# Sums of 32-row strips through DRAM, in place of one-hot matmuls, in a graph layer

## The chip, the cores and the metric

One core of a Trainium2 chip runs the kernel. The metric is the device time of one execution in microseconds (us).

## The reference

A graph layer over 6250 nodes and 206,250 edges (33 per node), D = 256, all in float32. The edges come sorted by their target node `dst`.

```python
h = relu(layernorm(x))                                   # [6250, 256]
e = relu(edge_attr[:, 1:] @ W_e1.T + b_e1) @ W_e2.T + b_e2
edge_emb = (e * (clip(edge_attr[:, 0:1], 0, 1) + 0.01)) @ W_le.T + b_le
msg = relu(h[src] + edge_emb)                            # per edge
aggr = segment_sum(msg, dst, 6250)                       # per node
y = (h + aggr) @ W_g1.T + b_g1
out = x + relu(layernorm(y) * ln_g + ln_b) @ W_g2.T + b_g2
```

## The kernel before

**Edges.** A tile is 128 edges. A block is S = 4 tiles, a half-block (the loop's unit `u`) two of them, a pair `q` two blocks. A group is L = 6 blocks, 3072 edges; its edges are laid out so that tile j of each of its blocks belongs to strip j, a run of 768 consecutive edges. The targets of such a run lie within W = 32 consecutive nodes. There are 67 full groups and at the end an odd one of one block (403 blocks, 806 half-blocks).

**Per half-block** the steps are these. `first_layer` (line 250) multiplies the edge features by `W_e1`, per pair; `edge_part` (L274) multiplies the result by the product of `W_e2` and `W_le`, and DVE copies it out as `msg` (L279). GpSimd (POOL) gathers the rows of `hb` = h + b_le by `src`, 128 rows in one indirect DMA (L566), two gathers per half-block, 1604 in the main part. `whole` multiplies `msg` by the polarity and adds the gathered rows (L615, DVE), then takes the relu (L620, ACT). `add_up` multiplies by 0/1 matrices `sel` (L632): strip j of the group is summed in partitions 32j to 32j+31 of an accumulator `pd`.

**Per group**, `keep` copies the accumulator to `ms` (L644, 128 rows x 256): 4 strips of 32 rows, each row the sum of one node over this group's edges.

**Per window** of 128 nodes (49 of them), `node_work` puts the groups' sums in their places and ends the layer. A window takes sums from two or three groups; there are 140 pairs of window and group. Its steps:

- `spread` loads x, x transposed (`hT`) and the rows' statistics (`stb`), and builds a one-hot matrix per group (L698); small steps on DVE turn `hT` into h (L707) and prepare `xt` (L211).
- `rows_of` (L732) multiplies each group's `ms` by its one-hot matrix, which gives the sums already transposed, and DVE adds h (L734).
- `one` is the product with `W_g1` (L170) and the normalisation, `two` the transposes (L186) and the relu (L189), `three` the product with `W_g2` (L196), the sum with x (L198) and the store (L201).

**Order.** The schedule is written by hand; each engine runs its instructions in the order in which the program emits them. The main loop counts half-blocks `u` from LEAD = 22 (22 are calculated before the first gather can run). `edge_part(u)` comes first; at each turn (every eight half-blocks) come `add_pairs` (all sums that are possible) and two `first_layer` calls and the raw loads of the pairs for the turn after (SP). `whole` follows `edge_part` at a distance `lag`, which starts at 18 half-blocks and gets shorter by one every 44. Node steps stand in `todo` with a due half-block, and `due` runs at most one per half-block.

**The gathers' account.** `in_step` books a fixed time for each step of PE and emits gathers as long as their number fits; the first of them waits for that step's last matmul (`behind`). What is still missing when `whole` needs it is emitted there, without such a wait.

```python
EDGE, LAYER, SUMS, NODES = 1.754, 0.9, 0.46, 0.65
STEP = 1.288
AFLOAT = 6.0
    spent += us
    while (got - 2 * RAW) * STEP < spent + AFLOAT and got < 2 * min(NU, 4 * summed + HG):
        gather(behind)
        behind = None
```

`EDGE` is booked per half-block, `LAYER` twice per `first_layer`, `SUMS` per block in `add_up`, `NODES` per step that `due` runs. `gathers(made + 1)` is the untied way.

**A fallback.** `verdict` and the steps around it test whether the targets lie as the layout assumes; if not, `any_order` computes everything again in a general way.

Of the kernel before, what the change touches and what calls it, by code (L numbers as in the profile page):

```python
# [17 lines left out]
P = 128  # L18
N = 6250
# [14 lines left out]
NB = NF * L + 1  # L34
NT = NB * S
NG = NF + 1
NP = -(-NB // 2)
MARGIN = 768
DEG = E // N
# [12 lines left out]
AHEAD = 10  # L52
assert DEG * N == E and NF * GE + S * P >= E


def group_of(b):
    return b // L


def blocks_of(g):  # L60
    return range(g * L, min((g + 1) * L, NB))


def windows_of(g):

    lo = (GE * g - MARGIN) // DEG
    hi = (GE * (g + 1) + MARGIN) // DEG
    return [w for w in range(NW) if w * P <= hi and (w + 1) * P > lo]
# [29 lines left out]
def gnn_kernel(ctx: ExitStack, tc: tile.TileContext, x, src_c, dst_c, dst_r, pol_c, raw_t, w_e1t, w_e2,  # L98
# [6 lines left out]
    st_d = dram.tile([NW, 2, P], F32, name="st_d")  # L105

# [42 lines left out]
    def finish_nodes(nd, ps, w, n):  # L149
# [3 lines left out]
        def turn(a):  # L153
# [3 lines left out]
            aT = nd.tile([P, 2, P], F32, name="aT")  # L157
# [7 lines left out]
        def first(aT, bias_by_pe=False):  # L165
            ph = ps()
            if bias_by_pe:
                nc.tensor.matmul(ph[:n, 0, :], ones[0:1, :n], bg1_b[0:1], start=True, stop=False)
            for c in range(2):
                nc.tensor.matmul(ph[:n, 0, :], aT[:, c, :n], wg1_s[:, c, :], start=c == 0 and not bias_by_pe, stop=c == 1)  # L170
            hs = nd.tile([P, D], F32, name="hs")
            if bias_by_pe:
# [7 lines left out]
            nc.vector.tensor_scalar(hs[:n], hb[:n], mv[:n, 0, 0:1], rs[:n], op0=ALU.subtract, op1=ALU.mult)  # L180
# [32 lines left out]
        return turn, first, second, third, load_x, offset  # L213
# [4 lines left out]
    with fast:  # L218
# [20 lines left out]
        def first_layer(q):  # L239

            bs = [b for b in (2 * q, 2 * q + 1) if b < NB]
# [97 lines left out]
        nc.gpsimd.iota(mid, pattern=[[GE, NG]], base=GE // 2, channel_multiplier=0, allow_small_or_imprecise_dtypes=True)  # L339
        p32 = const.tile([P, 1], F32, name="p32")  # L340
# [9 lines left out]
        full = NF * L * S  # L350
# [134 lines left out]
        def first_rows():  # L485

            pb = ps().rearrange("p a b -> p (a b)")[:, :NG * S].rearrange("p (g j) -> p g j", j=S)
            nc.tensor.matmul(pb[:, :NF, :], ones[0:1, :],
                             dst_f[0:1, :full].rearrange("o (g r) -> o g r", r=L * S)[:, :, :S], start=True, stop=True)
            nc.tensor.matmul(pb[:, NF, :], ones[0:1, :], dst_f[0:1, full:], start=True, stop=True)  # L490
            nc.scalar.activation(base_b, pb, AF.Copy)

        def rows_of_edges():
# [3 lines left out]
                base_b[:, :NF, :].rearrange("p g (o j) -> p g o j", o=1).to_broadcast([P, NF, L, S]), ALU.subtract)  # L497
            nc.vector.tensor_tensor(rel[:, full:], dst_f[:, full:], base_b[:, NF, :], ALU.subtract)
# [10 lines left out]
        def row_numbers():  # L509
            for j in range(S):  # L510
                q = slice(j * W, (j + 1) * W)
                nc.vector.tensor_scalar(rowid[q], base_b[q, :, j], p32[q], None, op0=ALU.add)


        far = w0.tile([P, 2, NG], F32, name="far")
        ends = w0.tile([P, 3], F32, name="ends")
        bad = w0.tile([P, 3], F32, name="bad")
        bad3 = w0.tile([3, 1], F32, name="bad3")

        def by_group(i, op):  # L520
            def step():
                nc.vector.tensor_reduce(far[:, i, :NF], dst_f[:, :full].rearrange("p (g r) -> p g r", r=L * S),
                                        axis=AX.X, op=op)
                nc.vector.tensor_reduce(far[:, i, NF:], dst_f[:, full:], axis=AX.X, op=op)
# [6 lines left out]

        def verdict():
            nc.vector.scalar_tensor_tensor(far[:, 0, :], far[:, 0, :], float(DEG), mid, op0=ALU.mult, op1=ALU.subtract)
            nc.vector.scalar_tensor_tensor(far[:, 1, :], far[:, 1, :], -float(DEG), mid, op0=ALU.mult, op1=ALU.add)
            nc.vector.tensor_reduce(ends[:, 2:3], far.rearrange("p a b -> p (a b)"), axis=AX.X, op=ALU.max)
            nc.vector.tensor_scalar(bad[:, 0:1], ends[:, 0:1], float(W - 1), None, op0=ALU.is_gt)
            nc.vector.tensor_scalar(bad[:, 1:2], ends[:, 1:2], 0.0, None, op0=ALU.is_lt)
            nc.vector.tensor_scalar(bad[:, 2:3], ends[:, 2:3], float(GE // 2 + MARGIN), None, op0=ALU.is_gt)

        def count():  # L540
            pq = ps()
            nc.tensor.matmul(pq[:3, 0, 0:1], bad, ones[:, 0:1], start=True, stop=True)
            nc.vector.tensor_copy(bad3, pq[:3, 0, 0:1])

        def total():
            pq = ps()
            nc.tensor.matmul(pq[:1, 0, 0:1], bad3, ones[0:3, 0:1], start=True, stop=True)
# [3 lines left out]
        with tc.tile_pool(name="hg", bufs=HG - RAW) as hg_p, tc.tile_pool(name="ms", bufs=5) as ms_p, \  # L551
                tc.tile_pool(name="sel2", bufs=9) as sel2_p, tc.tile_pool(name="nd", bufs=3) as nd:
# [6 lines left out]
            def gather(behind=None):  # L559

                nonlocal got
                u, i = divmod(got, 2)
                got += 1
                if i == 0:
                    hg[u] = (hx_p if u % HG < RAW else hg_p).tile([P, 2, D], F32, name="hg")
# [12 lines left out]
            def in_step(us, behind):  # L578
# [3 lines left out]
                while (got - 2 * RAW) * STEP < spent + AFLOAT and got < 2 * min(NU, 4 * summed + HG):  # L582
# [7 lines left out]
            def rows_of_block(g, k):  # L590

                t = (g * L + k) * S
# [7 lines left out]
            def piece():  # L600

                if steps and steps[0][0] <= now:
                    steps.popleft()[1]()
# [18 lines left out]
            def add_up(b):  # L622

                g = group_of(b)
                k = b - g * L
                if k == 0:
                    acc[g] = pd[:, g % 2, :] if g < NG - 1 else ps()[:, 0, :]
# [11 lines left out]
            def keep(g):  # L639

                if g is not None:
                    ms[g] = ms_p.tile([P, D], F32, name="ms")
                    if g != NG - 2:
                        nc.scalar.activation(ms[g], acc.pop(g), AF.Copy)  # L644
                    else:
                        nc.vector.tensor_copy(ms[g], acc.pop(g))
                    sel.pop(g)
                    for w in range(NW):
                        if groups_of(w)[-1] == g:
                            late.pop(w)()  # L650
                        elif groups_of(w)[-1] == g + 1 < NG - 1:
                            late[w] = node_work(w)

            def add_pairs(last=False):
# [3 lines left out]
                while summed < NP and min(4 * summed + 4, NU) < made + last:  # L658
                    for b in (2 * summed, 2 * summed + 1):
                        if b < NB:  # L660
                            whole_groups.append(add_up(b))
                            if b % L == 0 and group_of(b) + 2 < NG:
# [12 lines left out]
            ending = {-2: [], -1: []}  # L675
# [4 lines left out]
            def node_work(w, spread_now=False):  # L680
# [4 lines left out]
                far_apart = (3, 5, 4) if gs[-1] < NG - 3 else (2, 3, 2)  # L685
                turn, first, second, third, load_x, offset = finish_nodes(nd, ps, w, n)

                def spread():
                    box["xt"] = load_x()
                    box["hT"] = nd.tile([P, 2, P], F32, name="hT")  # L690
                    nc.sync.dma_start(out=box["hT"][:, :, :n], in_=x_t[:, :, w * P:w * P + n])
                    st = nd.tile([P, 2, P], F32, name="stb")
# [25 lines left out]

                def halves_out():
# [6 lines left out]
                def rows_of():  # L726
# [9 lines left out]
                    if gs[-1] < NG - 2:  # L736
                        at(now + far_apart[0], one)

                def one():
                    box["hs"] = first(box["hT"], gs[-1] >= NG - 2)  # L740
                    if gs[-1] < NG - 2:
                        at(now + far_apart[1], two)

                def two():
                    box["nT"] = second(box["hs"])
                    if gs[-1] < NG - 2:
# [9 lines left out]
                if gs[-1] < NG - 2:  # L756
                    return lambda: at(now + 2, rows_of)
                ending[gs[-1] - NG].append((sums_of, halves_out, rows_of, one, two, three, gs))
# [19 lines left out]
            for i, fn in ((0, first_rows), (1, strips), (5, row_numbers), (6, stats_out),  # L778
                          (8, node_weights)):
                at(LEAD + i, fn)  # L780
            for i, fn in enumerate((by_group(0, ALU.max), by_group(1, ALU.min), by_row(0, ALU.max), by_row(1, ALU.min),
                                    verdict, count, total)):
                at(LEAD + 22 + 5 * i, fn)
            flag = None
            for u in range(LEAD, NU):
                now = u
                forward(u)
# [7 lines left out]
                while made < ready_for:  # L795
                    gathers(made + 1)
                    whole(made)
                    made += 1
                due()
                if len(rest) > 6:  # L800
# [5 lines left out]
                if u == LEAD + 60:  # L806
                    flag = nc.values_load(bad_i[0:1, 0:1], min_val=0, max_val=3 * P)
# [4 lines left out]
            while steps:  # L812
                steps.popleft()[1]()
            before, last = ending[-2], ending[-1]
            for sums_of, halves_out, rows_of, one, two, three, gs in before:
                rows_of()
            for sums_of, halves_out, rows_of, one, two, three, gs in last:
                sums_of(gs[:-1])
            while made < NU:
                whole(made)  # L820
                made += 1
            for sums_of, halves_out, rows_of, one, two, three, gs in before:
                one()
            add_pairs(last=True)
            for sums_of, halves_out, rows_of, one, two, three, gs in last:
                sums_of(gs[-1:])
                halves_out()
            for sums_of, halves_out, rows_of, one, two, three, gs in before:
                two()
            for sums_of, halves_out, rows_of, one, two, three, gs in last:  # L830
                one()
            for sums_of, halves_out, rows_of, one, two, three, gs in before:
                three()
            for sums_of, halves_out, rows_of, one, two, three, gs in last:
# [10 lines left out]
def any_order(tc, dram, v):  # L845
# [7 lines left out]
    with tc.tile_pool(name="sc", bufs=1) as sc, tc.tile_pool(name="sk", bufs=2) as sk, \  # L853
# [78 lines left out]
        def nodes(w, n):  # L932
            ac = sk.tile([P, D], F32, name="ac_a")
            nc.sync.dma_start(out=ac[:n], in_=acc_d[bass.ds(w * P, n), :])
            turn, one, two, three, load_x, offset = v["finish_nodes"](sk, lambda: sp1.tile([P, 1, D], F32, name="ps_a"), w, n)
# [71 lines left out]
```

## Time and profile before

| | |
|---|---|
| median of 3 runs | 2162.19 us (2161.35 to 2164.05) |
| the profiled execution: its own time | 2161.02 us |
| its span, first to last instruction | 2159.3 us |
| granted TensorE clock, mean | 0.998 |
| PE (TensorE) busy | 2144.8 us |
| DVE (VectorE) busy | 1665.9 us |
| ACT (ScalarE) busy | 980.5 us |
| POOL (GpSimd) busy | 1621.5 us |
| DMA, mean rate | 143 GB/s |

A row of the profile gives line, engine, operation, out<-in by the program's names, the number of instructions, then busy time and the mean of one in ns, then the engine's idle time ahead of them and what ended it. PEld is the weight load. Names with a q (SPq, POOLq) are queues: instructions that issue DMAs or wait. In a row of a line with times by stretch, the columns are the stretch, its length, the busy time with the number of instructions, the granted clock, the DMA engines' share and GB/s. A float32 matmul stands as two instructions, a transpose as one.

### The profile page before, as it was taken

The numbers are of one execution on the slowest core, as the hardware profiler recorded it, in microseconds if no ns is written. First come the engines' busy times: TensorE is split into PE (matmuls) and PEld (weight loads), VectorE is DVE, ScalarE is ACT, GpSimd is POOL, SyncE is SP. The second block draws the span as 40 slices with busy tenths as digits, with TensorE's granted clock in tenths as the row PEclk, the third lists the DMA queues.
The fourth block names the chain that finished last, engine by engine and source line by source line (L and its number), as shares of the span: only waits on it lengthen the run. The fifth ranks groups of instructions, "written<-read, shape, count | busy, mean of one in ns | idle before, by whom it ended". The sixth has DMA issues, their size and how long they took to land.

```text
span 2159.3 us, 35666 instructions
## 1 busy us (share of the span) xinstructions
PE 2144.8 (99%) x12382; PEld 1613.3 (75%) x12382; DVE 1665.9 (77%) x3975; ACT 980.5 (45%) x1710; POOL 1621.5 (75%) x1675
## 2 busy tenths in 40 slices
PE   9999999999999999999999999999999999999998
PEld 6677777777777777777777777777777777777776
DVE  7898777877777777777777777778777778777786
ACT  7544444444444444444444444444444444444443
POOL 6777777777777777777777777777777777777773
PEclk9999999999999999999999999999999999999999
DMA  9544454544445454545454445444544554454442
GB/s 312 175 134 127 141 157 135 150 137 131 140 131 148 144 149 125 152 131 149 124 151 142 133 130 153 143 133 141 147 138 125 150 151 140 128 152 131 140 138 73
DMA packets 156227, 309.23 MB, mean 143 GB/s; under 512 B 33328, under 2 KB 78089, under 8 KB 156041
## 3 DMA queue, kind: packets, MB, share of 16 engines
q0 software_dynamic: 77376, 211.39, 34.6%
q1 hardware_dynamic: 77364, 92.23, 13.6%
q10 hardware_dynamic: 1300, 3.28, 0.5%
q8 instruction: 98, 1.61, 0.3%
q14 instruction: 89, 0.72, 0.1%
HBM read 293.92 MB, written 12.85 MB: 142 GB/s over the span
## 4 chain that ended last, share of the span: by engine, by line
PE 96%; DVE 2%; DMA 1%; ACT 0%; issue 0%; SPq 0%; DVEq 0%; ACTq 0%
PE pz L274 64%; PE pz L250 17%; PE pd L632 9%; PE pz L732 3%; PE pz L170 2%; PE pz L196 2%; DMA raw<-in_raw_t_dram 1%; PE pz L186 1%; DVE hg L615 0%; DVE msg L279 0%; DVE st L141 0%; DMA xt<-in_x_dram 0%; DVE sel L595 0%; DVE mvx L142 0%; DVE msg L613 0%
## 5 line engine op out<-in xcount | busy, mean ns | idle before, releaser
L566 POOL DMA_INDIRECT hg<-hb_d,src_s x1604 | 1576.6, 983 | 493.9 <-issue 319.8
L274 PE MATMUL pz<-wc_s,e 128*128 128x256 f32 x6448 | 1452.6, 381 | 0.0
L274 PEld LDWEIGHTS pz<-wc_s,e 128*128 128x128 f32 x6448 | 1209.5, 190 | 235.2 <-ACT e L259 71.3
L620 ACT ACTIVATE hg<-hg 128x512 f32<-128x512 f32 x805 | 507.6, 631 | 862.7 <-DVE hg L615 860.9
L615 DVE SCALAR_TENSOR_TENSOR hg<-msg,pol_s,hg 128x256 f32<-128x256 f32 x1612 | 696.8, 477 | 15.6 <-DMA hg<-hb_d,src_s 14.9
L279 DVE TENSOR_TENSOR msg<-pz,bc_s 128x512 f32<-128x512 f32 x799 | 545.5, 683 | 74.0 <-PE pz L274 73.7
L256 DVE TENSOR_SCALAR e<-pz,vecs 128x512 f32<-128x512 f32 x201 | 150.8, 750 | 361.1 <-PE pz L250 361.0
L259 ACT ACTIVATE e<-pz,vecs 128x512 f32<-128x512 f32 x605 | 361.1, 691 | 148.4 <-PE pz L250 148.3
L250 PE MATMUL pz<-raw,we_s 64*128 64x512 f32 x1612 | 379.3, 604 | 3.7 <-DVE msg L279 2.0
L250 PEld LDWEIGHTS pz<-raw,we_s 64*128 64x128 f32 x1612 | 148.5, 187 | 188.2 <-issue 155.4
L632 PE MATMUL pd<-hg,sel 128*32 128x256 f32 x3216 | 194.9, 382 | 0.6 <-ACT hg L620 0.6
L632 PEld LDWEIGHTS pd<-hg,sel 128*32 128x32 f32 x3216 | 94.4, 109 | 87.8 <-issue 34.9
L595 DVE SCALAR_TENSOR_TENSOR sel<-iota_w,zero_c,rel 128x128 f32<-128x128 f32 x403 | 137.3, 341 | 0.0
L644 ACT ACTIVATE ms<-pd 128x256 f32<-128x256 f32 x66 | 25.2, 382 | 127.2 <-PE pd L632 127.1
L732 PEld LDWEIGHTS pz<-s,ms 128*128 128x128 f32 x548 | 68.7, 192 | 3.1 <-PE pd L632 0.4
L732 PE MATMUL pz<-s,ms 128*128 128x128 f32 x548 | 69.3, 275 | 0.1
L707 DVE SCALAR_TENSOR_TENSOR hT<-hT,zero_c,stb 128x128 f32<-128x128 f32 (+1 forms) x196 | 66.7, 341 | 3.0 <-DMA stb<-st_d 3.0
L196 PE MATMUL pz<-wg_s,nT 128*128 128x256 f32 (+1 forms) x196 | 50.6, 380 | 0.6 <-ACT nT L189 0.6
L170 PE MATMUL pz<-wg_s,hT 128*128 128x256 f32 (+1 forms) x196 | 50.5, 380 | 0.0
L392 POOL TENSOR_TENSOR hb<-xt,rows_b 128x256 f32<-128x256 f32 (+1 forms) x49 | 34.1, 728 | 10.5 <-ACT xt L388 3.0
L196 PEld LDWEIGHTS pz<-wg_s,nT 128*128 128x128 f32 (+1 forms) x196 | 37.0, 190 | 6.2 <-ACT nT L189 0.8
L170 PEld LDWEIGHTS pz<-wg_s,hT 128*128 128x128 f32 (+1 forms) x196 | 37.0, 190 | 5.7 <-issue 0.3
(98 smaller groups left out, 412.8 us busy)
## 6 DMA issues: line engine op xcount, KB each, us to landing
raw<-in_raw_t_dram SPq DMA_DIRECT2D x202, 256.0 KB
hg<-hb_d,src_s POOLq DMA_INDIRECT x1604
stb<-st_d SPq DMA_DIRECT2D x49, 128.0 KB
hb_d<-hb SPq DMA_DIRECT2D x12, 512.0 KB
xt<-in_x_dram SPq DMA_DIRECT2D x48, 128.0 KB
hT<-in_x_t_dram SPq DMA_DIRECT2D x48, 128.0 KB
out_dram<-ot SPq DMA_DIRECT2D x48, 128.0 KB
xt<-in_x_dram SPq DMA_DIRECT2D x11, 512.0 KB
```

Source lines behind the costliest of these rows:

```text
L196: nc.tensor.matmul(po[:n, 0, :], nT[:, c, :n], wg2_s[:, c, :], start=c == 0, stop=c == 1)
L250: z = nc.tensor.matmul(pe[s, c], we1_s[s * F:(s + 1) * F, c * P:(c + 1) * P], raw[q][s * F:(s + 1) * F, :], start=True, stop=True)
L256: nc.vector.tensor_scalar(e1[b][:, c, :], pe[s, c], be1_s[:, c:c + 1], 0.0, op0=ALU.add, op1=ALU.max)
L259: nc.scalar.activation(e1[b][:, c, :], pe[s, c], AF.Relu, bias=be1_s[:, c:c + 1])
L274: last_z = nc.tensor.matmul(pz[:, i, :], e1[b][:, c, k:k + P], wc_s[:, c, :], start=c == 0, stop=c == 1)
L279: nc.vector.tensor_add(msg[u], pz, bc_s)
L566: g = nc.gpsimd.indirect_dma_start(out=hg[u][:, i, :], out_offset=None, in_=hb_d, in_offset=bass.IndirectOffsetOnAxis(ap=src_s[:, 2 * u + ...
L595: nc.vector.scalar_tensor_tensor(sel[g][:, k * S:(k + 1) * S, :], iota_w.rearrange("p (o w) -> p o w", o=1).to_broadcast([P, S, W]), zero_ ...
L615: nc.vector.scalar_tensor_tensor(hg[u][:, i, :], m[:, i, :], pol_s[:, 2 * u + i:2 * u + i + 1], hg[u][:, i, :], op0=ALU.mult, op1=ALU.add)
L620: nc.scalar.activation(hg[u], hg[u], AF.Relu)
L632: z = nc.tensor.matmul(acc[g][j * W:(j + 1) * W, :], sel[g][:, k * S + j, :], m[:, j % 2, :], start=k == 0, stop=b == blocks_of(g)[-1])
L732: nc.tensor.matmul(pa[:, c, :n], ms[g][:, c * P:(c + 1) * P], box["sel2"][i][:, :n], start=i == 0, stop=i == len(gs) - 1)
```

## The change

Two things change.

**Sums through DRAM.** For the windows whose last group is before the odd one (47 of 49), `rows_of` and its one-hot matrices go. Two DRAM tables `sum_d[0]`, `sum_d[1]` of N + 32 rows are cleared window by window (`clear`). After a group's copy, `rows_out` loads the first node numbers of its four strips into SP's registers and stores the strips to these rows, even strips in one table and odd ones in the other. `far_work` takes the place of `node_work`: x is loaded, ACT computes h (`load`), SP loads 128 rows of both tables, DVE adds them (`add`, twice), `turned` transposes on PE and copies out on ACT; `one`, `two` and `third` follow as before. `turned`, `one`, `two` and `third` are run by `due`; the rest isn't: SP's part is started by `moves` at fixed distances of 1 to 8 half-blocks.

**The odd group.** The block of the odd group moves ahead of the last full group, next to a void block (VOID) that is skipped everywhere; 404 blocks, 808 half-blocks in number, 806 of them computed. At the end only the last window is left; its first groups' sums and its bias are begun ahead of the last blocks.

The test gets one more condition (strips two apart don't overlap). EDGE, LAYER, SUMS, NODES, STEP, AFLOAT, `lag` and `due` stay as they are. The core of the diff:

```diff
+CLEAR = 4
 def group_of(b):
-    return b // L
+    return b // L if b < VOID else NG - 1
...
+    sum_d = [dram.tile([N + W, D], F32, name=f"sum_d{i}") for i in range(2)]
...
+            nc.vector.tensor_copy(base_i, base_b[0:1].rearrange("p g j -> p (g j)"))
...
             def gather(behind=None):
                 nonlocal got
+                if got == 4 * VOID:
+                    got += 4
...
-                while (got - 2 * RAW) * STEP < spent + AFLOAT and got < 2 * min(NU, 4 * summed + HG):
+                while (got - 4 * (got > 4 * VOID) - 2 * RAW) * STEP < spent + AFLOAT and got < 2 * min(NU, 4 * summed + HG):
...
             def keep(g):
...
                     sel.pop(g)
+                    if g < FAR:
+                        soon(1, lambda: rows_out(g, 0))
+                        soon(2, lambda: rows_out(g, 1))
                     for w in range(NW):
-                        if groups_of(w)[-1] == g:
+                        if groups_of(w)[0] == g + CLEAR:
+                            soon(6, lambda w=w: clear(w))
+                        if groups_of(w)[-1] == g < FAR:
+                            far_work(w)
+                        elif groups_of(w)[-1] == g:
                             late.pop(w)()
...
+            def soon(n, fn):
+                moves.setdefault(now + n, []).append(fn)
+
+            def clear(w):
+                if groups_of(w)[-1] < FAR:
+                    for i in range(2):
+                        nc.sync.dma_start(out=sum_d[i][w * P:(w + 1) * P, :], in_=zrow)
+
+            def rows_out(g, k):
+                if k == 0:
+                    _, firsts[g] = nc.values_load_multi_w_load_instructions(
+                        base_i[0:1, g * S:(g + 1) * S], engines=[mybir.EngineType.SP], min_val=0, max_val=N)
+                for i in range(2):
+                    j = 2 * k + i
+                    nc.sync.dma_start(out=sum_d[i][bass.ds(firsts[g][j], W), :], in_=ms[g][j * W:(j + 1) * W, :])
+
+            def far_work(w):
+                box = {}
+                turn, bias, first, second, third, load_x, offset = finish_nodes(nd, ps, w, P)
+                def h_of_x():
+                    box["xt"] = load_x()
+                    box["h"] = nh.tile([P, 2, P], F32, name="stb").rearrange("p a b -> p (a b)")
+                def load():
+                    nc.scalar.activation(box["h"], box["xt"], AF.Relu, bias=nm_s[:, w:w + 1], scale=rs_s[:, w:w + 1])
+                    box["ab"] = ab_p.tile([P, 2, D], F32, name="ab")
+                    for i in range(2):
+                        nc.sync.dma_start(out=box["ab"][:, i, :], in_=sum_d[i][w * P:(w + 1) * P, :])
+                def add(i):
+                    nc.vector.tensor_add(box["h"], box["h"], box["ab"][:, i, :])
+                def turned():
+                    box["hT"] = turn(box["h"], nh, "hT")
+                    at(now + 2, one)
+                def one():
+                    box["hs"] = first(box["hT"])
+                    at(now + 5, two)
+                def two():
+                    box["nT"] = second(box["hs"])
+                    at(now + 4, lambda: third(box["nT"], box["xt"]))
+                soon(1, h_of_x)
+                soon(4, load)
+                steps.extend((now + 6, lambda i=i: add(i)) for i in range(2))
+                steps.extend((now + 7, lambda c=c: offset(box["xt"], c)) for c in range(2))
+                at(now + 9, turned)
...
             for u in range(LEAD, NU):
                 now = u
-                forward(u)
+                if u == NU - 1:
+                    whole(made)
+                    made += 1
+                if u // 2 != VOID:
+                    forward(u)
...
                 due()
+                for fn in moves.pop(now, []):
+                    fn()
...
+            for begin, sums_of, halves_out, one, two, three, gs in ending:
+                begin()
+            while made < NU:
+                whole(made)
+                made += 1
...
+            add_pairs(last=True)
+            for begin, sums_of, halves_out, one, two, three, gs in ending:
+                sums_of(gs[-1:])
+                halves_out()
+                one()
```

More of the change, by code (lines that the diff above doesn't have):

```diff
@@ L37 @@
 NP = -(-NB // 2)
+FAR = NG - 2
 MARGIN = 768
+SP = S * P
+LAST = 512
+VOID = (NF - 1) * L + 1
 DEG = E // N
@@ L211, in offset @@
             nc.vector.scalar_tensor_tensor(xt[:n, h], xt[:n, h], zero_c[:n], bg2_b[:n, h], op0=ALU.add, op1=ALU.add)
-        return turn, first, second, third, load_x, offset
+        return turn, bias, first, second, third, load_x, offset
     NU = 2 * NB
@@ L600, in piece @@
             def piece():
-                if steps and steps[0][0] <= now:
-                    steps.popleft()[1]()
+                due_now = [s for s in steps if s[0] <= now][:1]
+                if due_now:
+                    steps.remove(due_now[0])
+                    due_now[0][1]()
                 elif rest:
@@ L806, in gnn_kernel @@
                 if u == LEAD + 60:
-                    flag = nc.values_load(bad_i[0:1, 0:1], min_val=0, max_val=3 * P)
+                    flag = nc.values_load(bad_i[0:1, 0:1], min_val=0, max_val=4 * P)
+            assert not moves
+            while steps:
+                steps.popleft()[1]()
+            for begin, sums_of, halves_out, one, two, three, gs in ending:
+                begin()
+            while made < NU:
+                whole(made)
+                made += 1
+            for now in sorted(todo):
+                for fn in todo.pop(now):
+                    fn()
+            add_pairs(last=True)
[3 more added lines that the diff above has]
+                one()
             while todo:
@@ L811, in gnn_kernel @@
                     fn()
[L812 to L834, printed above, removed]
+            for begin, sums_of, halves_out, one, two, three, gs in ending:
                 two()
```

167 lines of the change are left out of this document (107 added, 60 removed).

## The prediction

> **What bounds the kernel now.** I read the page first (the shares of the engines, the chain that ended last), then the groups of instructions by line, then one line alone (the gathers) with its table by stretches, then the timeline at the places that carry a price.
>
> ```profile
> span 2159.3 us, 35666 instructions
> PE 2144.8 (99%) x12382; PEld 1613.3 (75%) x12382; DVE 1665.9 (77%) x3975; ACT 980.5 (45%) x1710; POOL 1621.5 (75%) x1675
> PE 96%; DVE 2%; DMA 1%; ACT 0%; issue 0%; SPq 0%; DVEq 0%; ACTq 0%
> PE pz L274 64%; PE pz L250 17%; PE pd L632 9%; PE pz L732 3%; PE pz L170 2%; PE pz L196 2%; DMA raw<-in_raw_t_dram 1%; PE pz L186 1%; DVE hg L615 0%; DVE msg L279 0%; DVE st L141 0%; DMA xt<-in_x_dram 0%; DVE sel L595 0%; DVE mvx L142 0%; DVE msg L613 0%
> ```
>
> By the page TensorE (PE) is the bound: busy for 99% of the span and 96% of the chain. GpSimd (POOL) seems to have a quarter to spare. Its one large line says otherwise:
>
> ```profile
> L566 POOL DMA_INDIRECT hg<-hb_d,src_s x1604 | 1576.6, 983 | 493.9 <-issue 319.8 <-PE pz L274 41.2 <-ACT hg L620 32.9
> L566 POOL DMA_INDIRECT hg<-hb_d,src_s x1604: 942/946/1963, 65.3 to 2131.8; - x179
> 100.00:200.00 100.00, 76.55 (x78) 1.00 0.49 142
> 1200.00:1300.00 100.00, 76.23 (x79) 1.00 0.46 133
> 2000.00:2100.00 100.00, 75.91 (x78) 1.00 0.48 141
> 263.08 0.94 POOL L566 DMA_INDIRECT hg<-hb_d,src_s  x1 [0.30 <-PE pz L196]
> 265.86 0.48 DVE L615 SCALAR_TENSOR_TENSOR hg<-msg,pol_s,hg 128x256 f32<-128x256 f32 x1 [0.77 <-DMA hg<-hb_d,src_s]
> 2131.85 0.95 POOL L566 DMA_INDIRECT hg<-hb_d,src_s  x1 [0.30 <-issue]
> ```
>
> The first gather starts at 65.3 us, the last ends at 2131.85 + 0.95 = 2132.8. That is 2067.5 us for 1604 gathers, 1.289 us each, and 78 or 79 of them in every 100 us, early and late. The idle time of 493.9 us is 0.308 us a gather, and 0.30 stands ahead of a gather even where nothing held it (the last row); only some 10 us of it can be waiting. So POOL is full as well, from 65.3 to 2132.8. The kernel has two full engines, and the page's share hides the second because the gap of 0.30 isn't counted as busy. A faster PE alone can't move the end of the gathers.
>
> The Trainium skill, "Trainium Kernel Development and Optimization" (Performance Expectations), says that matmul busy time tells badly how near a kernel is to its limit and that LDWEIGHTS busy is the better measure. Here that is 75% beside 99%, so by that rule a cut on PE is worth less than its own length; by PE's 99% it is worth all of it (the third rival). The gathers' rows agree with the rule.
>
> **PE: what goes and what comes.** A window of 128 nodes now costs a one-hot matmul per group that reaches into it. In the code there are 140 such pairs; 47 windows with 134 of the pairs take the new path, and the last two windows keep the old one.
>
> ```profile
> L732 PE MATMUL pz<-s,ms 128*128 128x128 f32 x548 | 69.3, 275 | 0.1
> 1005.94 1.93 PE L632 MATMUL pd<-hg,sel 128*32 128x256 f32 x32
> 1007.80 3.70 PE L250 MATMUL pz<-raw,we_s 64*128 64x512 f32 x16
> 1011.44 3.72 PE L274 MATMUL pz<-wc_s,e 128*128 128x256 f32 x16
> 1015.00 1.50 PE L732 MATMUL pz<-s,ms 128*128 128x128 f32 x12
> 1016.33 5.35 PE L274 MATMUL pz<-wc_s,e 128*128 128x256 f32 x24
> 1036.71 0.38 PE L186 MATMUL pz<-ident,hs 128*128 128x128 f32 x2
> 1036.93 1.89 PE L274 MATMUL pz<-wc_s,e 128*128 128x256 f32 x8
> ```
>
> Twelve instructions (three groups) take the stream from 1015.00 to 1016.33: 0.111 us each. 134 pairs are 536 instructions: 59.4 us go. Two transposes a window come; two of them take from 1036.71 to 1036.93, 0.22 us: 47 x 0.22 = 10.3 us. PE gets 49 us shorter. The edge matmuls, the first layer and the strips' sums are the same in number (the void block is skipped), and so are the 1604 gathers.
>
> **DVE, ACT and SP.**
>
> ```profile
> L615 DVE SCALAR_TENSOR_TENSOR hg<-msg,pol_s,hg 128x256 f32<-128x256 f32 x1612 | 696.8, 477 | 15.6 <-DMA hg<-hb_d,src_s 14.9
> L707 DVE SCALAR_TENSOR_TENSOR hT<-hT,zero_c,stb 128x128 f32<-128x128 f32 (+1 forms) x196 | 66.7, 341 | 3.0 <-DMA stb<-st_d 3.0
> L698 DVE TENSOR_SCALAR s<-iota_p,rowid 128x128 f32<-128x128 f32 x140 | 31.6, 289 | 0.0
> L734 DVE SCALAR_TENSOR_TENSOR hT<-hT,pz 128x256 f32<-128x256 f32 x48 | 19.6, 409 | 0.0
> L388 ACT ACTIVATE xt<-xt,nm_s,rs_s 128x256 f32<-128x256 f32 (+1 forms) x49 | 25.4, 590 | 7.1 <-DVE nm_s L385 6.9
> L644 ACT ACTIVATE ms<-pd 128x256 f32<-128x256 f32 x66 | 25.2, 382 | 127.2 <-PE pd L632 127.1
> L620 ACT ACTIVATE hg<-hg 128x512 f32<-128x512 f32 x805 | 507.6, 631 | 862.7 <-DVE hg L615 860.9 <-DVE ot L198 1.5 <-DVE bad L543 0.3
> SPq L201 <- DVE ot L198: 1383.9, 48, 36.6
> L807 SPq TENSOR_LOAD <-bad_i x1: 485/485/485, 216.8 to 216.8; - x1
> L807 SPq FUSED_REGOPS  x1: 181/181/181, 217.3 to 217.3; - x1
> L201 SPq DMA_DIRECT2D out_dram<-ot x49: 333/344/344, 195.3 to 2154.0; - x49
> ```
>
> DVE loses 188 x 0.34 (L707) + 134 x 0.23 (L698) + 47 x 0.41 (L734) = 114 us and gains 94 additions of 128x256; the nearest row is L615, 696.8/1612 = 0.43 us, so 41 us: 73 us less on an engine that isn't the bound. ACT gains 47 x (0.59 + 0.38) = 46 us (a relu like L388, a copy out of PSUM like L644) and had 45%. Both cost nothing while PE and POOL are full.
>
> SP gets, for each of 66 groups, four register loads (0.49 + 0.18 us each, row L807) and four stores (0.34 each), and per window two clears and two loads of sums in place of two other loads. On SP's queue a store now waits for the group's sums, and loads of sums wait for stores. Queued behind it stand the raw loads, whose users come eight half-blocks later (a half-block is 256 edges, two gathers, 2.6 us; so 21 us); SP already sits in such waits for 1383.9 us. The chain from a group's copy to the loaded sums, with the landing time below for each transfer that waits for another: 0.4 + 2.7 + 0.7 + 1.8 + 0.7 + 1.8 + 0.9 + 1.8 = 10.8 us; DVE adds six half-blocks, 15.6 us, after it. Cover of 5 us: I take no cost. Without it DVE stalls, and that is a rival.
>
> **The step that decides: what paces the gathers.** A gather is put into POOL's program by an account: each PE step books a fixed time (1.754 per half-block, 0.9 twice per pair, 0.46 per block, 0.65 per node step), and gathers are emitted, tied to that PE step, as long as their number x 1.288 is under the account + 6. What a half-block then still lacks is emitted on the spot, untied. Booked per half-block: 1.754 + 0.45 + 0.23 = 2.434, and five node steps per window of 16.5 half-blocks, 0.197: 2.631/1.288 = 2.043 gathers. Needed: 2 x (1 + 1/44) = 2.045, as the lag shrinks by one in 44. The account just keeps up. At half-block 300 it has 278 x 2.631 + 7.8 (twelve single steps) = 739, so 8 + 745/1.288 = 587 gathers against 2 x (283 + 6) = 578 needed: 9 ahead.
>
> The change leaves EDGE, STEP and the rest as they are, but a far window has four node steps, not five. Booked: 2.592, 2.012 gathers. The lead of 9 shrinks by 0.031 per half-block, and about half-block 320 it is gone. PE itself got faster by 49 us, so it comes up against gathers that are late already, and at a turn (every eight half-blocks: sums, then first layers) the next gather is tied to a first-layer matmul that stands behind sums that wait for the gathers before. The loop, from the end of one gather to the release of the next: landing 1.8 us (263.08 + 0.94 to 265.86; that DVE step reads this gather), L615 twice 0.9, L620 0.63, four blocks' sums 1.87 (1005.94 to 1007.80), a quarter of the first layers 0.9: 6.1 us. The one half-block by which the lag is longer ahead of a turn, and what the untied emission adds, give POOL two to four gathers in the meantime, 2.6 to 5.2 us. It idles for 0.9 to 3.5 us a turn, and 6 at most with no cover; I take 2.4, a little over the middle as single turns go without.
>
> How many turns: within eight half-blocks the lead swings by (1.84 + 3.6 + 1.75)/1.288 - 2 = 3.6 gathers, a step of the lag takes 2 at once, rounding 1. The stretch from the first shortage to the point where every gather is emitted untied (and so isn't held any more) is 6.6/0.031 = 213 half-blocks, 27 turns, about half-blocks 210 to 430, 0.6 to 1.2 ms in the time line. 27 x 2.4 = 65 us of idle POOL. Afterwards POOL is full again but can't win it back: its own 1.289 us is the bound.
>
> **The end.**
>
> ```profile
> 2143.45 0.87 DVE L615 SCALAR_TENSOR_TENSOR hg<-msg,pol_s,hg 128x256 f32<-128x256 f32 x2
> 2153.52 0.42 DVE L198 TENSOR_TENSOR ot<-pz,xt 106x256 f32<-106x256 f32 x1 [2.00 <-PE pz L196]
> ```
>
> The last half is used at 2143.9, 11.1 us after its gather ended, though 1.8 would do: PE was late. With a faster PE up to 9.2 us of the 26.5 us after the last gather go. I take 20 us (the last group is now a full one and its last pair is summed there; the window before the last one is done ahead). Sum: 2132.8 + 65 + 20 = 2218 us of span; the profiled execution took 2161.0 for a span of 2159.3, and the median is 1.2 over it: **2221 us**.
>
> **Rivals.**
> *The pace doesn't bite* (gathers wait in POOL's queue long enough ahead, and the ties are met in time). POOL stays full: 2132.8 + 17.5 to 20 + 2.9 = 2153 to 2156 us, slightly faster. For it: no gather of before stood waiting. Against: the account above. It decides for this case if the loss of the lead costs under 0.3 us a turn.
> *PE's clock falls in the stalls.*
>
> ```profile
> 80.00:85.00 5.00, 4.28 (x10) 0.66 0.35 98
> 80.72 2.25 PE L250 MATMUL pz<-raw,we_s 64*128 64x512 f32 x4 [1.51 <-DVE msg L279]
> ```
>
> After a gap of 1.51 us the granted clock was 0.66 over 5 us: 1.7 us lost. At 27 turns that adds 46 us: 2267. The Trainium skill, "TensorE: Matmul & The Clock Gate" (HAM oscillation), puts the limit at idle gaps of over about 3.4 us, under which few of my stalls would count; the row shows a shorter one doing it, though beside another gap.
> *PE's whole cut comes out:* 2162 - 49 - 4 = 2109. It needs gathers at 0.946 + 0.305 = 1.25 us throughout, and the stretches show 1.28.
> *The sums come late through DRAM.* If the chain on SP is 8 us longer than I have it, DVE stands 3 us in each of 47 windows with everything behind it: 2162 + 141 = 2303, or more on top of the pace. Against: cover of 5 us.
>
> **How the numbers follow.** The pace 0.58, the pace with the clock 0.10, no bite 0.18, the whole cut 0.05, late sums 0.09. The likeliest case alone runs from 27 x 1 to 27 x 4 us: 2183 to 2264. The range takes in no bite below and the clock's middle above: 2150 to 2268, leaving out about 0.2. A measurement can tell 0.2%, 4 us. Slower 0.58 + 0.10 + 0.09 = 0.77; of no bite 0.15 counts as faster and 0.03 as the same; faster 0.15 + 0.05 = 0.20.
>
> **What would show it.** The gathers by 100 us: 78 until about 600 us, some 70 to 73 between 700 and 1300, 78 again after; their idle time up from 494 to about 560 us, with first-layer matmuls as releasers of gaps of 1 us and more; the last gather starting near 2197. PE busy near 2096, DVE 1593, ACT 1026, twelve-instruction groups of one-hot matmuls left only at the end, transposes at 0.11 us each. DVE waiting for gathers far more than 14.9 us. I am wrong if gathers stay at 78 all the way (no bite), if they rise to 80 (the whole cut), or if DVE waits long for loads of sums.

## The result, and the profile after

The changed kernel took 2240.88 us (median; 2237.96 to 2244.82) against 2161.95 us for the kernel before: a ratio of 1.0364, 95% interval [1.0344, 1.0384]. The forecast was 2221 us, in the range of 2150 to 2268.

First the page of the changed kernel: span, engines, chain.

```profile
span 2241.0 us, 36002 instructions
PE 2154.2 (96%) x11940; PEld 1581.0 (71%) x11940; DVE 1634.9 (73%) x3712; ACT 1008.0 (45%) x1805; POOL 1605.0 (72%) x1677
PE 35%; issue 4%; POOL 3%; DMA 2%; DVE 1%; ACT 1%; POOLq 0%; ACTq 0%
```

PE has 442 instructions fewer (12382 to 11940: 536 go, 94 come), as forecast, and PEld, the weight load, is 32 us shorter. But PE busy went up by 9 us, so busy time isn't work done. The first layer shows it, with the same 1612 instructions (L250 before, L268 now; busy time and mean ns, then idle time):

```profile
L250 PE MATMUL pz<-raw,we_s 64*128 64x512 f32 x1612 | 379.3, 604 | 3.7 <-DVE msg L279 2.0 <-DMA raw<-in_raw_t_dram 1.6
L268 PE MATMUL pz<-raw,we_s 64*128 64x512 f32 x1612 | 408.2, 613 | 19.8 <-DVE msg L297 18.7 <-DMA raw<-in_raw_t_dram 0.7 <-DVE st L155 0.2
```

No engine has a larger share of the span than before. The chain has only 35% on PE, and its parts add up to less than half of the span, so little is read from it.

Now the gathers (L615 here, L566 before). Their row in the page's costliest groups (busy time and mean ns, then idle time ahead of them):

```profile
L615 POOL DMA_INDIRECT hg<-hb_d,src_s x1604 | 1560.0, 973 | 601.4 <-issue 373.2
```

The same line by itself (shortest, median and longest ns, first and last start):

```profile
L615 POOL DMA_INDIRECT hg<-hb_d,src_s x1604: 940/946/2067, 63.6 to 2221.2; - x179
```

And its table by stretch (POOL busy and gathers, granted clock of PE, DMA's share, GB/s):

```profile
500.00:600.00 100.00, 76.24 (x79) 1.00 0.52 152
600.00:700.00 100.00, 73.43 (x78) 1.00 0.52 155
700.00:800.00 100.00, 65.92 (x70) 0.97 0.42 124
...
1000.00:1100.00 100.00, 61.36 (x64) 0.96 0.39 115
...
1300.00:1400.00 100.00, 65.06 (x67) 0.93 0.41 120
1400.00:1500.00 100.00, 76.21 (x79) 1.00 0.50 149
...
2100.00:2200.00 100.00, 76.24 (x79) 1.00 0.50 147
```

Up to 700 us 78 or 79 gathers run in 100 us, from 700 to 1400 us 64 to 73, and then 79 again. The loss lies in one stretch, and the full rate afterwards doesn't win it back. The seven stretches hold 472 gathers, where 79 each would be 553: 81 are missing, 104 us at 1.289. The account of the span closes: the first gather starts 1.7 us sooner (65.3 to 63.6), the gathers themselves are 16.6 us shorter in sum (1576.6 to 1560.0), their idle time is 107.5 us longer (493.9 to 601.4). So the last one ends at 2222.4, not 2132.8 (2221.2 and the 1.22 us of the row below). After it the span has 18.6 us left, not 26.5. Together 81.7 us more, the difference of the two spans.

How the loss looks from inside, in the timeline of the changed kernel (start, length, idle time before and what ended it):

```profile
1131.39 1.93 PE L683 MATMUL pd<-hg,sel 128*32 128x256 f32 x32
1136.31 1.05 POOL L615 DMA_INDIRECT hg<-hb_d,src_s  x1 [2.07 <-issue]
1139.58 0.95 POOL L615 DMA_INDIRECT hg<-hb_d,src_s  x1 [2.21 <-PE pz L268]
1150.94 2.08 PE L187 MATMUL pz<-wg_s,hT 128*128 128x256 f32 x4 [6.04 <-ACT hT L173]
1162.03 1.93 PE L683 MATMUL pd<-hg,sel 128*32 128x256 f32 x32
1163.89 3.70 PE L268 MATMUL pz<-raw,we_s 64*128 64x512 f32 x16
1166.66 0.94 POOL L615 DMA_INDIRECT hg<-hb_d,src_s  x1 [8.22 <-ACT e L277]
...
2221.21 1.22 POOL L615 DMA_INDIRECT hg<-hb_d,src_s  x1 [0.30 <-issue]
```

This is one turn: the sums (L683) at 1131.39 and again at 1162.03, 30.6 us apart, where eight half-blocks of gathers take 16 x 1.289 = 20.6. In between PE stands for 6.04 us ahead of the product with `W_g1` (L187), because the copy of the transposed sums (L173) is late on ACT. In ACT's program this copy stands behind three relus (L671); the trace has them at 1143.34, 1145.58 and 1149.98, each after a wait for DVE's addition of gathered rows, and the copy at 1150.52. So PE comes late to everything that follows, the sums at 1162.03 among it, ahead of which it doesn't stand at all. Then POOL stands for 8.22 us and goes on 2.8 us after the first layer's matmuls begin at 1163.89. Each waits for the other: PE for work that needs gathers, POOL for the PE step to which its next gather is tied.

The view of the waits, by engine and line (total, times, longest), changed kernel; the last two rows are from SP's own view:

```profile
DVE hg L666 <- DMA hg<-hb_d,src_s: 349.2, 429, 2.9
POOL hg L615 <- PE pz L268: 61.9, 80, 9.4
POOL hg L615 <- ACT e L277: 51.1, 71, 8.2
PE pz L187 <- ACT hT L173: 47.0, 23, 6.4
PE pz L268 <- DVE msg L297: 18.7, 21, 1.5
PE pd L683 <- ACT hg L671: 3.2, 4, 1.0
SPq L756 <- DMA sum_d<-ms: 74.7, 61, 2.8
SPq L771 <- DMA sum_d<-ms: 67.2, 64, 2.0
```

And the group of DVE's additions that use the loaded sums, in the table by line:

```profile
L774 DVE TENSOR_TENSOR stb<-stb,ab 128x256 f32<-128x256 f32 x94 | 39.3, 418 | 0.9 <-DMA ab<-sum_d 0.9
```

Gaps of up to 9.4 us ahead of gathers end with the first layer (L268), as the prediction has it. But PE hardly waits at the sums (3.2 us, L683), where the prediction put its wait; it waits at the product with `W_g1` and for DVE's copies `msg` (L297), which stand behind the additions of late gathers. The sums' way through DRAM does make SP wait (stores for stores, L756; loads for stores, L771), but DVE waited for loaded sums only 0.9 us in all (the end of this row).

### The profile page after: what moved, and what is told of

It reads as the page before. It is cut to its first block, busy times and chain, and to the rows that moved or that the text cites. A ratio compares the mean times of both kernels' runs of the same rounds, so it can differ in the third digit from the quotient of the medians.

```text
span 2241.0 us, 36002 instructions
## 1 busy us (share of the span) xinstructions
PE 2154.2 (96%) x11940; PEld 1581.0 (71%) x11940; DVE 1634.9 (73%) x3712; ACT 1008.0 (45%) x1805; POOL 1605.0 (72%) x1677
## 5 line engine op out<-in xcount | busy, mean ns | idle before, releaser
L615 POOL DMA_INDIRECT hg<-hb_d,src_s x1604 | 1560.0, 973 | 601.4 <-issue 373.2
L292 PE MATMUL pz<-wc_s,e 128*128 128x256 f32 x6448 | 1464.9, 383 | 0.0
L292 PEld LDWEIGHTS pz<-wc_s,e 128*128 128x128 f32 x6448 | 1219.4, 192 | 240.5 <-ACT e L277 73.6
L671 ACT ACTIVATE hg<-hg 128x512 f32<-128x512 f32 x805 | 507.7, 631 | 1108.4 <-DVE hg L666 1105.4
L666 DVE SCALAR_TENSOR_TENSOR hg<-msg,pol_s,hg 128x256 f32<-128x256 f32 x1612 | 732.1, 480 | 354.5 <-DMA hg<-hb_d,src_s 349.2
L297 DVE TENSOR_TENSOR msg<-pz,bc_s 128x512 f32<-128x512 f32 x799 | 543.3, 683 | 16.4 <-PE pz L292 16.0
L268 PE MATMUL pz<-raw,we_s 64*128 64x512 f32 x1612 | 408.2, 613 | 19.8 <-DVE msg L297 18.7
L268 PEld LDWEIGHTS pz<-raw,we_s 64*128 64x128 f32 x1612 | 157.5, 187 | 222.5 <-issue 115.6
L683 PE MATMUL pd<-hg,sel 128*32 128x256 f32 x3224 | 199.5, 382 | 3.3 <-ACT hg L671 3.2
L683 PEld LDWEIGHTS pd<-hg,sel 128*32 128x32 f32 x3224 | 95.4, 109 | 93.8 <-issue 35.0
L187 PE MATMUL pz<-wg_s,hT 128*128 128x256 f32 (+1 forms) x196 | 59.2, 429 | 48.4 <-ACT hT L173 47.0
L187 PEld LDWEIGHTS pz<-wg_s,hT 128*128 128x128 f32 (+1 forms) x196 | 36.7, 204 | 65.0 <-ACT hT L173 58.2
L774 DVE TENSOR_TENSOR stb<-stb,ab 128x256 f32<-128x256 f32 x94 | 39.3, 418 | 0.9 <-DMA ab<-sum_d 0.9
L207 ACT ACTIVATE nT<-pz,vecs 128x128 f32<-128x128 f32 (+1 forms) x98 | 38.6, 443 | 1.4 <-PE pz L204 1.4
L229 DVE SCALAR_TENSOR_TENSOR xt<-xt,zero_c,rows_b 128x128 f32<-128x128 f32 (+1 forms) x98 | 33.6, 343 | 0.0
```

What stands on the lines that cost most here:

```text
L268: z = nc.tensor.matmul(pe[s, c], we1_s[s * F:(s + 1) * F, c * P:(c + 1) * P], raw[q][s * F:(s + 1) * F, :], start=True, stop=True)
L292: last_z = nc.tensor.matmul(pz[:, i, :], e1[b][:, c, k:k + P], wc_s[:, c, :], start=c == 0, stop=c == 1)
L297: nc.vector.tensor_add(msg[u], pz, bc_s)
L615: g = nc.gpsimd.indirect_dma_start(out=hg[u][:, i, :], out_offset=None, in_=hb_d, in_offset=bass.IndirectOffsetOnAxis(ap=src_s[:, 2 * u + ...
L666: nc.vector.scalar_tensor_tensor(hg[u][:, i, :], m[:, i, :], pol_s[:, 2 * u + i:2 * u + i + 1], hg[u][:, i, :], op0=ALU.mult, op1=ALU.add)
L671: nc.scalar.activation(hg[u], hg[u], AF.Relu)
```

## The experiments

Three theories. P, the pace: the account is short by one node step per window, and where tied and untied gathers mix, POOL and PE wait for each other. D: the way of the sums through DRAM is the cost. H, the hand-over: PE waits for the transposed sums because the product stands two half-blocks behind.

**The missing bookings put back.**

```diff
-EDGE, LAYER, SUMS, NODES = 1.754, 0.9, 0.46, 0.65
+EDGE, LAYER, SUMS, NODES = 1.754, 0.9, 0.46, 0.85
```

> Changed kernel with NODES 0.85 for 0.65: four node steps book what five booked before. Theories: P, the pace (the account runs short, and gathers tied to PE steps behind late sums leave POOL idle); D, the sums' way through DRAM (SP's register loads, stores and clears, more traffic); H, the hand-over (PE waits at the W_g1 product for the copy of the transposed sums, 47.0 us in the changed kernel, because it stands two half-blocks behind). P: booked 2.434 + 4 x 0.85/16.5 = 2.640, 2.050 gathers per half-block against 2.045 needed, so the lead holds, gathers run at 1.289 us throughout, the last ends near 2133 us, 2150 to 2158 us in all. D: 2235 to 2245, since nothing on SP or in DRAM changes. H: 2230 to 2245, the distance stays two half-blocks.

Measured: 2142.28 us, ratio 0.9907 [0.9891, 0.9924]. Of its page, the engines and the gathers' group:

```profile
PE 2114.6 (99%) x11940; PEld 1563.1 (73%) x11940; DVE 1626.1 (76%) x3712; ACT 1010.1 (47%) x1805; POOL 1615.0 (75%) x1677
...
L615 POOL DMA_INDIRECT hg<-hb_d,src_s x1604 | 1569.9, 979 | 493.7 <-issue 337.1
```

The gathers' first and last start, and then one stretch in the middle of the former loss (from 200 to 2100 us every 100 us hold 78 or 79):

```profile
L615 POOL DMA_INDIRECT hg<-hb_d,src_s x1604: 942/949/2067, 63.3 to 2123.4; - x179
```

```profile
1100.00:1200.00 100.00, 76.21 (x79) 1.00 0.51 146
```

The idle time is 493.7 us again (493.9 in the kernel before) and the stretch of the loss is gone. This kernel and the changed one differ in the bookings alone, so the 98.6 us between them need the shortage, and D, which is in both, doesn't cause them. It came out 8 us under P's lower end, because the last gather ended at 2124.6 and not at 2133.

**Bookings taken away.** The same line with 0.0.

> Changed kernel with NODES 0: node steps book nothing, the account is short far earlier. P: booked 2.434, 1.890 gathers per half-block, a shortage of 0.156 each; the stretch in which tied and untied gathers mix is 6.6/0.156 = 42 half-blocks, 5 or 6 turns at the 3.5 to 4 us a turn that the changed kernel shows: about 20 us of idle POOL, 2170 to 2185 us, thus faster than with 0.65. If a short account alone made it slow (without the mix of tied and untied), slower than 2240. D and H: 2235 to 2245.

Measured: 2164.96 us, 1.0019 [1.0009, 1.0029]. With no bookings for node steps at all the kernel is 76 us faster than with 0.65. A poor account alone isn't what costs. The time is 5 us under P's range; against e1 it is 22.7 us more, and the gathers' idle time is 514.8 us, 21 more, as P had it. P's range stood on 2150 for the kernel without loss, where e1 measured 2142.

**Ties taken away.**

```diff
-                    gather(behind)
+                    gather()
```

> Changed kernel, no gather is tied to a PE step any more; the account and the order of emission stay. P: as in e1, POOL runs through at 1.289 us: 2150 to 2158 us. D and H: 2235 to 2245.

Measured: 2145.13 us, 0.992 [0.9903, 0.9937]; idle time 491.8 us (the gathers' group):

```profile
L615 POOL DMA_INDIRECT hg<-hb_d,src_s x1604 | 1574.1, 981 | 491.8 <-issue 346.3
```

The account is as short here as in the changed kernel. Without the tie to a PE step it does no harm. The time is 5 us under P's range, for the same reason as in e1.

**The shortage put into the kernel before.** NODES 0.52, so that five steps book what the changed kernel's four book.

> Kernel before with NODES 0.52 for 0.65: its five node steps book what the changed kernel's four book (2.6 us a window); no sums go through DRAM and no hand-over of transposed sums is in it. P: the same shortage, 2220 to 2270 us, with the gathers' rate falling between 0.6 and 1.4 ms. D and H: 2162, as nothing that they name is in this kernel.

Measured: 2240.18 us, 1.0366 [1.0349, 1.0383], with one-hot matmuls, without any sums in DRAM and without the copy of transposed sums on ACT (here DVE's addition L734 stands in its place). That this is also the changed kernel's time to the microsecond is chance. The loss is what counts: 2240.18 - 2160.86 = 79.3 us here, against 98.6 us for the same shortage in the changed kernel. Its gathers by stretch, and PE's wait at the product with `W_g1` (L170 here), 5.0 us where the changed kernel has 47.0:

```profile
700.00:800.00 100.00, 65.45 (x68) 1.00 0.41 118
...
1100.00:1200.00 100.00, 59.99 (x63) 0.93 0.40 119
...
1300.00:1400.00 100.00, 76.24 (x79) 1.00 0.48 140
```

```profile
PE pz L170 <- DVE hT L734: 5.0, 3, 2.5
```

From 700 to 800 us 68 gathers run at a granted clock of 1.00: eleven are lost there without any loss of clock.

**The hand-over one half-block later.**

```diff
                     box["hT"] = turn(box["h"], nh, "hT")
-                    at(now + 2, one)
+                    at(now + 3, one)
```

> Changed kernel (NODES 0.65) with the W_g1 product three half-blocks behind the transposes, not two; the account books the same. P: the ties and the shortage stay, POOL still idles at the turns; the wait of 47.0 us for the copied sums goes, but PE then waits somewhere else in the same loop: 2215 to 2245 us. If the hand-over is a cause of its own beside the pace: its 47.0 us go, 2185 to 2200 us.

Measured: 2220.62 us, 1.0276 [1.0258, 1.0293]. The wait at the product with `W_g1`, in the view of the waits:

```profile
PE pz L187 <- ACT hT L173: 15.4, 8, 4.4
```

31.6 us of this wait went, and the ratio fell from 1.0364 to 1.0276, about 19 us. The time lies within P's range, but H isn't nothing. With the hand-over one half-block later some 78 us of loss are left (2220.62 - 2142.28), about the 79.3 us that the same shortage costs in the kernel before. So of the 98.6 us about 20 need the hand-over as well as the shortage, and the rest comes without it. With enough bookings the same wait is 13.0 us (e1); whether the later hand-over would win something there as well wasn't run.

**More bookings in the kernel before.** NODES 0.85 there.

> Kernel before with NODES 0.85: its account gets richer, nothing else. P: POOL was full already and PE's last part sets the end, so 2156 to 2166 us, no change; what e1 won over the kernel before (18 us) comes from PE's shorter work and not from the account. If the richer account is itself the gain: about 2142.

Measured: 2161.04 us, 0.9999 [0.999, 1.0009]. What e1 wins over the kernel before comes from the change, not from the richer account. The change has two parts, the sums through DRAM and the odd group's new place, and no run has only one of them; which part wins how much stays open.

**Fewer gathers in the train.** e1 with

```diff
-RAW = 4
-HG = 16 + RAW
+RAW = 6
+HG = 14 + RAW
-AHEAD = 10
+AHEAD = 9
-        ... tc.tile_pool(name="p1x", bufs=11) as p1x:
+        ... tc.tile_pool(name="p1x", bufs=10) as p1x:
```

> e1 with six half-blocks, not four, gathered straight from x at the start (RAW 6, ring of 20 gather buffers kept, one buffer less for loading x). P: POOL is the bound of e1, and four gathers fewer stand in its train after the nodes' rows are written: 4 x 1.285 = 5 us less, 2136 to 2139. If the loads of x that now run one buffer less ahead start the train later, or PE is the bound of e1: 2141 to 2150.

Measured: 2140.24 us, 0.9903 [0.9887, 0.992]. The interval overlaps with that of e1, so the two aren't told apart, and the median lies between the two expectations (2136 to 2139, 2141 to 2150), so it decides for neither. In its profile the last of 1600 gathers starts at 2117.5 us, against 2123.4 for the last of 1604 in e1. It is the lowest median here; e1 and it are about 0.9% faster than the kernel before.

**How long the mixed stretch is.** The changed kernel with NODES 0.70 and 0.50.

> Changed kernel with NODES 0.70. P with the length of the mixed stretch as the prediction worked it: booked 2.434 + 4 x 0.70/16.5 = 2.604, 2.0215 gathers, 0.024 short of 2.045 a half-block; 6.6/0.024 = 276 half-blocks, 34 turns against 27 at 0.65. The changed kernel lost 2240.9 - 2142.3 = 98.6 us against e1, 3.65 a turn; 34 turns are 124 us: about 2266, slower than with 0.65 though the account is richer. If the loss goes simply with the account's shortage: less than 2240, some 2215.

> Changed kernel with NODES 0.50. P as for 0.70: booked 2.555, 1.984 gathers, 0.0615 short; 6.6/0.0615 = 107 half-blocks, 13 turns, 13 x 3.65 = 49 us: about 2191. If the loss goes simply with the account's shortage: about 2310.

These two took 2752.47 and 3139.53 us, but the kernel before took 2592.4 us beside them, not 2161. By ratio (1.0607 and 1.2075) 0.50 is the slower one there, against what P says. In the trace of 0.50 PE stands for 284.7 us ahead of `edge_part` (L292) with no releaser to be seen, where the same kernel has 0.0 us below. What slowed them isn't known, so neither theory is judged by them. The same two kernels follow beside a kernel before of 2161.57 us.

> The same kernel as e8_credit70 (NODES 0.70), again, as the kernel before took 2592 us beside it and 2161 beside all others. P: 34 turns x 3.65 us, about 2266 us, slower than with 0.65. If the loss goes simply with the account's shortage: some 2215.

> The same kernel as e9_credit50 (NODES 0.50), again for the same reason. P: 13 turns x 3.65 us, about 2191 us. If the loss goes simply with the account's shortage: about 2310.

Measured: 2344.73 us with 0.70 (1.0848 [1.0829, 1.0866]) and 2184.93 us with 0.50 (1.0109 [1.0092, 1.0126]). From 0 over 0.50, 0.65 and 0.70 to 0.85 the ratios are 1.0019, 1.0109, 1.0364, 1.0848 and 0.9907: the nearer the account comes to enough, the worse, until it is enough. That is what a stretch of length 6.6/shortage gives, and a loss in step with the shortage doesn't. The gathers of the 0.70 kernel by stretch:

```profile
1000.00:1100.00 100.00, 75.61 (x78) 1.00 0.54 162
...
1500.00:1600.00 100.00, 62.70 (x67) 0.93 0.44 128
...
2100.00:2200.00 100.00, 60.42 (x64) 0.91 0.39 115
2200.00:2300.00 100.00, 76.23 (x79) 0.97 0.48 138
```

The stretch runs here from about 1100 to 2200 us. The trace has 44 turns in it, where 34 were worked out, and its price a turn is higher too: 2344.7 - 2142.3 = 202 us, 4.6 us a turn. 0.50 came within 6 us of its expectation, 0.70 was 79 us above it. In the trace of 0.50 gaps stand from about 275 to 620 us, 15 turns where 13 were worked out, at 42.6 / 15 = 2.8 us: part of the close hit is luck, as the expectation took 3.65. So the length of the stretch follows 6.6/shortage roughly, and the price a turn, taken as fixed, grew with the length in these three kernels (2.8, 3.4 and 4.6 us). (The expectations set the shortage against 2.045, the prediction against 2.043; against 2.043 the turns would be 38 and 14.)

## Why the prediction was right, step by step

- **Two full engines.** Right. In e1 PE's work is shorter (weight load 1613.3 to 1563.1, 50 us) and the time falls by 18.6 us only, with the gathers end to end: the last one ends 8.2 us sooner, and the rest is behind it. PE still shows 99% there, so the share of busy matmuls misled, and the weight load's 73% did not. That is the rule of the Trainium skill, "Trainium Kernel Development and Optimization" (Performance Expectations), named in the prediction.
- **The cut on PE, 49 us.** Its size fits the weight load's 50 us; "PE busy near 2096" was wrong (2154.2, and 2114.6 in e1): busy time is no measure of the work cut, as the first layer's 379.3 and 408.2 us for the same instructions show. DVE 1634.9 and ACT 1008.0 were forecast as 1593 and 1026; neither decided.
- **DRAM costs nothing.** Right: 0.9 us of waits, and e1 with all its stores and loads is the faster kernel.
- **The account.** Right in direction, and nearly in place: the gathers fall back from about 700 us and run at the full rate from 1400 (forecast 0.6 to 1.2 ms). Shown by e1 (account filled), e3 (ties gone) and e4 (the shortage without the change).
- **The loop at a turn.** Half right. The tie is as forecast: most of the long gaps of the gathers end with the first layer. But PE hardly waits for gathers at the sums (3.2 us in all). PE is held at the product with `W_g1` (47.0 us) and by DVE's copies (18.7 us), neither of which the loop names, and then works its way to the tie while POOL stands.
- **The idle time: 27 x 2.4 = 65 us.** The mis-sized term. It measured 107.5 us. The stretch from 0.7 to 1.4 ms holds 472 gathers, 16 to a turn, thus 29 turns, so the number of turns (27) held; the price was 107.5 / 29 = 3.7 us a turn, beyond the 3.5 that I took for its upper end with cover. It isn't even: gaps of over 0.45 us hold 33 us beyond the usual 0.30 in the 13 turns before 1000 us, 2.5 us a turn as forecast, and 73 us in the 16 turns after it, 4.5 us a turn. There single gaps pass the 6.1 us that I had for a loop without any cover:

```profile
1262.61 3.70 PE L268 MATMUL pz<-raw,we_s 64*128 64x512 f32 x16
1266.62 0.94 POOL L615 DMA_INDIRECT hg<-hb_d,src_s  x1 [9.35 <-PE pz L268]
```

This gather goes 4.0 us after the first layer begins and the one at 1166.66 goes 2.8 us after it; the loop had 0.9 for that. About 20 of the 98.6 us go with the hand-over (e5, e4). Why the loss grows along the stretch isn't settled. The clock can have a part in it: the mean granted clock is 0.987, against 0.997 in e1, which is at most some 23 us over the span (an estimate from the two means and spans, idle time of PE included). It isn't needed for a loss, since the kernel before with 0.52 loses eleven gathers in 100 us at a clock of 1.00, and no run held the clock apart from the waits.

- **The end, 20 us.** It measured 18.6 us.
- **Not foreseen:** the gathers' own time fell by 16.6 us (and by 6.7 in e1); a rate of 1.289 was taken as fixed. It is most of why e1's last gather ended 8.2 us sooner than that of the kernel before, and with that of why e1 came out 11 us under the floor of the rival "the pace doesn't bite" (2153). In the changed kernel it hid part of the idle time in the total: idle time 42 us above the forecast, gathers 17 us below, and so 2241 us lies only 20 us from 2221. That much of the nearness is luck.

## What to carry to other kernels

An engine that is idle for the same short time ahead of every instruction (0.30 us here) can be full, whatever its share says: count instructions per 100 us over the run before believing that a cut elsewhere pays. Where a hand-written schedule books fixed times per step to pace another queue, removing a step takes its booking away too; work out supply and demand of the queue again with each change of the steps. A tie that only paces should fall away as soon as it is late. Here an account that is nearly enough was the worst of all (2345 us at 0.70), and no tie at all was within 3 us of the best booking.

## What the runs showed of the hardware that was not expected

A gather takes 0.946 us at the median, but the mean moved between 973 ns (changed kernel) and 988 ns (the kernel before with NODES 0.85), without a change in the gathers:

```profile
L566 POOL DMA_INDIRECT hg<-hb_d,src_s x1604 | 1584.0, 988 | 492.8 <-issue 351.9
```

Over 1604 gathers these 15 ns are 24 us, more than e1's whole gain. The kernels that lose gathers lie at 972 to 977 ns, the others at 976 to 988. What moves it wasn't tried.

The granted clock fell below 1.00 in all stretches from 700 to 1400 us of the changed kernel, down to 0.93, and to 0.91 in the last such stretch shown of the 0.70 kernel. In the turn of the timeline above, by 2.5 us (PE busy and instructions, granted clock, DMA's share, GB/s):

```profile
1145.00:1147.50 2.50, 0.00 (x0) 0.89 0.91 239
1147.50:1150.00 2.50, 0.00 (x0) 0.50 0.65 234
1150.00:1152.50 2.50, 1.56 (x4) 0.50 0.33 98
1152.50:1155.00 2.50, 2.50 (x10) 0.74 0.37 105
1155.00:1157.50 2.50, 2.50 (x13) 1.00 0.36 105
```

Within the one gap of 6.04 us (up to 1150.94) the clock goes to 0.50, and it is back at 1.00 from 1155 us on. The four matmuls with `W_g1` behind the gap take 2.08 us; at 1252.02, without a gap, the same step takes 1.03. So a single late copy costs PE the wait and some of the time after it.
